# Layer 1's preparation in a four-layer graph network: fillings for TensorE, and the order of DVE's and GpSimd's first work

## The chip, the cores and the metric

One core of a Trainium2 chip runs the whole program in one launch. The time is device microseconds (us) of that core; a smaller number is better. Engines are called PE or TensorE (matrix products), DVE or VectorE, ACT or ScalarE, POOL or GpSimd, and SP, which issues most DMAs.

## The reference, cut to what matters

x has 3327 nodes of 64 values, adj is 3327 x 3327. Four layers follow one another, each ending in a layer norm of x plus the layer's result. Layer 1, where the change lies:

```python
x = _layernorm(x + _L0_gnn_ref(L0_gnn_t, x, adj))           # layer 0: leaves a centred, scaled x
# layer 1
x_tan = _logmap0(x, C)
left  = x_tan @ att_W[:D] + att_b
right = x_tan @ att_W[D:]
adj_att = sigmoid(left + right.T) * adj                      # N x N
x_local = _logmap(x[:, None, :], x[None, :, :], C)           # N x N x 64, never formed by the kernel
support_t = einsum('ij,ijd->id', adj_att, x_local)
x = _layernorm(x + _proj(_expmap(x, support_t, C), C))
# layer 2: two rounds of tanh([adj @ x, x] @ W); layer 3: a ranked, decayed neighbour sum
```

For an x whose rows all have enough variance, layer 0's result lies at one distance from the origin. The kernel then takes the logarithm as a cubic in one product of rows, so that layer 1 is, for every pair of a block of neighbours j and a chunk of nodes i: a product of rows (pq), a sigmoid times adj, the cubic, and a second product that sums over j.

## The kernel before, in words

The nodes are padded to 26 blocks of 128 and paired into 13 "slots by two": block b lies in slot 2b for b below 13, and block b + 13 in slot 2b + 1. A tile [128, 26, 64] holds one row of 64 per node and slot.

**Preparation, first part** (lines 918 to 1008, in an order written out by hand for all engines). DVE sums and centres x (xc). TensorE turns x to columns (pt_x) and multiplies each pair of blocks by the centred attention weights, so pr holds each node's left and right term; the 13 products lie in four groups of 4, 4, 4 and 1 (`turned`). Between them stand products whose result nobody reads, the fillings (`idle`, an identity times a matrix of 128x512 or 128x256). n_low counts rows with a low variance. DVE copies it to `flag`; every engine loads the flag and branches on it (lines 1819 and 1820) before layer 1's main part. DVE also forms lf (left), rb (right plus bias), s, ga, gas and others, each [128, 26]. GpSimd has put x minus its last column into lj.

**Preparation, second part** (`near_sphere`, from line 1244, again in a written order). DVE multiplies rows of lj by s (`scaled`, which takes b and n and does slots 2b to 2(b + n)), and makes the rows ri (`rows_of_i`). TensorE turns lf, lj and ri into columns, in tiles of PSUM, and ScalarE or DVE copies them out: `left` gives lb, a row of lf on all partitions; `right` gives ljT[0]; `wrong` gives the other half order ljT[1]; `turn` gives riT. `bank` and `alone` issue TensorE's instructions at once and return the function that copies. The tile `after` is a copy of one column that GpSimd makes so as to wait for DVE.

**Main loop.** 52 pairs of a j block and a half of the columns, each in two steps, 104 steps in all. `attention` makes a sigmoid on ScalarE (L1076) and its product with adj on GpSimd (L1088); the very first pair is done in two halves, and `next(start)` issues the first. `products` makes pq (L1103) three steps ahead; `linear` makes a on DVE (L1115) and a square on ScalarE (L1116); `gather` makes v on DVE (L1124) and sums on TensorE (L1133). One step thus needs two DVE instructions, one square, half a sigmoid, half a GpSimd product and eight TensorE records.

The blocks of adj come by DMA on SP's queue: four of them are kept in SBUF from the start, the others pass through a ring of four.

In the first part the lines that the change touches are 977 to 1008, in the second 1262 to 1275:

Of the kernel before, what the change touches and what calls it, by code (L numbers as in the profile page):

```python
# [10 lines left out]
F32 = mybir.dt.float32  # L11
# [4 lines left out]
ALU = mybir.AluOpType  # L16
# [3 lines left out]
P = 128  # L20
N = 3327
NB = 26
NP = NB * P
D = 64
# [34 lines left out]
LOG_NORM = float(np.arctanh(np.float64(ATANH_MAX)))  # L59
# [17 lines left out]
def kernel(  # L77
# [11 lines left out]
    nc = tc.nc  # L89
# [14 lines left out]
    ident = const.tile([P, P], F32, name="ident")  # L104
    make_identity(nc, ident)
    lj = const.tile([P, NB, D], F32, name="lj")
# [9 lines left out]
    ones = const.tile([P, 1], F32, name="ones")  # L116
# [4 lines left out]
    attb_sb = const.tile([P, 1], F32, name="attb_sb")  # L121
# [69 lines left out]
    center_4 = center.unsqueeze(1).to_broadcast([P, 4, P])  # L191
# [705 lines left out]
    with tc.tile_pool(name="l1", bufs=1) as l1:  # L897

        def l1_stat(name):
# [6 lines left out]
        s, inv_s, gas, dl, al, xf, lf, rb = (  # L906
            l1_stat(name) for name in ("s", "inv_s", "gas", "dl", "al", "xf", "lf", "rb")
        )
# [4 lines left out]
        r2 = l1.tile([P, 2, NB], F32, name="r2")  # L913
        flag = l1.tile([1, 1], I32, name="flag")
        xc = xpool.tile([P, NB, D], F32, tag="x", name="xc")
        vec, sca = nc.vector.tensor_tensor, nc.vector.tensor_scalar
        stt = nc.vector.scalar_tensor_tensor
        with tc.tile_pool(name="l1a", bufs=1) as l1a, tc.tile_pool(
            name="l1ap", bufs=1, space=PSUM
        ) as l1ap:  # L920
            v = l1a.tile([P, NB], F32, name="v")
            sums = l1a.tile([P, NB], F32, name="sums")
            sq = l1a.tile([P, NB, D], F32, name="sq_c")
            xT = l1a.tile([P, HALF], F32, name="xT_0")

            idle = l1ap.tile([P, 4 * P], F32, name="idle")
            for _ in range(3):
                nc.tensor.matmul(idle, ident, center_4, start=True, stop=True)  # L928

            pw = l1ap.tile([P, 4], F32, name="pw")  # L930
            attw_c = l1a.tile([P, 4], F32, name="attw_c")
            halves = (slice(0, None, 2), slice(1, None, 2))
            for h in halves:
                nc.vector.tensor_reduce(sums[:, h], x0[:, h, :], axis=AX.X, op=ALU.add)
            for h in halves:
                stt(
                    xc[:, h, :], sums[:, h].unsqueeze(2).to_broadcast([P, NBH, D]), -1.0 / D,
                    x0[:, h, :], op0=ALU.mult, op1=ALU.add,
                )
            for h, c in zip(halves, (x0, xc)):  # L940

                nc.gpsimd.tensor_tensor(
                    lj[:, h, : D - 1], c[:, h, : D - 1],
                    c[:, h, D - 1 : D].to_broadcast([P, NBH, D - 1]), ALU.subtract,
                )

            pr = l1ap.tile([P, NBH, 2, 2], F32, name="pr")
            turned = []
            for i, g in enumerate(range(0, NBH, 4)):
                n = min(4, NBH - g)  # L950
                pt = l1ap.tile([P, 4 * P], F32, tag="pt", bufs=4, name=f"pt_x_{g}")
                for k in range(n):
                    nc.tensor.transpose(
                        pt[:, k * P : (k + 1) * P],
                        by_half(x0)[:, g + k].rearrange("p h d -> p (h d)"), ident,
                    )
                if i == 1:
                    nc.tensor.matmul(pw, center, attw_dg, start=True, stop=True)
                    nc.scalar.copy(attw_c, pw)
                    for h in halves:  # L960
                        nc.scalar.activation(sq[:, h, :], xc[:, h, :], AF.Square)
                nc.scalar.copy(xT[:, g * P : (g + n) * P], pt[:, : n * P])
                turned.append((g, n))
            for h in halves:
                nc.vector.tensor_reduce(v[:, h], sq[:, h, :], axis=AX.X, op=ALU.add)
            sca(vq[:, 1], v, 0.81 / D, LN_EPS, ALU.mult, ALU.add)
            sca(vq[:, 0], v, MIN_VAR, None, ALU.max)
            sca(vq[:, 2], v, 0.81 / D - 0.81, LN_EPS, ALU.mult, ALU.add)

            low = stat("low")  # L970
            stt(low, v, NEAR_VAR, real, op0=ALU.is_lt, op1=ALU.mult)
            lows = small.tile([P, 1], F32, tag="lows", name="lows")
            nc.vector.tensor_reduce(lows, low, axis=AX.X, op=ALU.add)
            root = l1a.tile([P, 2, NB], F32, name="root")
            n_low = l1ap.tile([1, 1], F32, name="n_low")
            for i, (g, n) in enumerate(turned):
                if i == 3:
                    nc.tensor.matmul(n_low, lows, ones, start=True, stop=True)
                for k in range(g, g + n):
                    nc.tensor.matmul(  # L980
                        pr[:, k].rearrange("p h t -> p (h t)"), xT[:, k * P : (k + 1) * P],
                        attw_c, start=True, stop=True,
                    )
                if i in (0, 3):
                    w = 2 if i else 4
                    nc.tensor.matmul(
                        idle[:, : w * P], ident, center_4[:, :w], start=True, stop=True
                    )
            nc.scalar.activation(root, vq[:, :2], AF.Sqrt)
            nc.scalar.activation(warm, ones, AF.Sigmoid)  # L990
            nc.vector.reciprocal(root, root)
            t = l1a.tile([P, 2, NB], F32, name="t")
            vec(t, vq[:, :2], root, ALU.mult)
            nc.vector.tensor_copy(flag, n_low)
            vec(t, t, root, ALU.mult)
            stt(r2, t, -3.0, root, op0=ALU.add, op1=ALU.mult)
            prs = pr.rearrange("p n h t -> p (n h) t")
            stt(lf, prs[:, :, 0], -0.5 * LOG_NORM, r2[:, 0], op0=ALU.mult, op1=ALU.mult)
            stt(rb, prs[:, :, 1], -0.5 * LOG_NORM, r2[:, 0], op0=ALU.mult, op1=ALU.mult)

            nc.vector.reciprocal(rq, vq[:, 1:])
            sca(rb, rb, attb_sb, None, ALU.add)
            sca(s, r2[:, 1], -0.45, None, ALU.mult)
            vec(g1, vq[:, 2], rq[:, 0], ALU.mult)
            vec(ga, vq[:, 1], rq[:, 1], ALU.mult)
            sca(aa, g1, -1.0, 1.0, ALU.mult, ALU.add)
            vec(gas, ga, s, ALU.mult)
            sca(lj[:, :, D - 1], aa, 1.0, None, ALU.add)
        in_order.close()

        def near_sphere(mT, ljT_0, xm, sq_e, t_e, rows_63):
# [3 lines left out]
            with tc.tile_pool(name="n1", bufs=1, reuse_waits="tile") as n1, tc.tile_pool(  # L1015
                name="n1w", bufs=2, reuse_waits="tile"
            ) as n1w, tc.tile_pool(
                name="n1c", bufs=1, space=PSUM, reuse_waits="tile"
            ) as n1c, ExitStack() as pairs:
                first_ps = ExitStack()  # L1020
                n1p = first_ps.enter_context(
                    tc.tile_pool(name="n1p", bufs=1, space=PSUM, reuse_waits="tile")
                )
# [4 lines left out]
                ri = mT.rearrange("p (n d) -> p n d", d=D)  # L1028
# [171 lines left out]
                def made(pt, make, b, n, at_once=True):  # L1200
                    dst, src = make(pt, b, n)

                    def copy(to=nc.scalar.copy):
                        to(dst, src)
                        if make is right and b < 9:
                            if at_once:
                                change_over(b, n)
                            else:
                                changes.append((b, n))

                    return copy
# [20 lines left out]
                def alone(make, b, n):  # L1232

                    pt = n1p.tile([P, 4 * P], F32, name=f"first_{make.__name__}_{b}")
                    return made(pt, make, b, n)

                with tc.manual_schedule(
# [7 lines left out]
                    def scaled(b, n):  # L1245

                        sl = slice(2 * b, 2 * (b + n))
                        vec(
                            lj[:, sl, : D - 1], lj[:, sl, : D - 1],
                            s[:, sl].unsqueeze(2).to_broadcast([P, 2 * n, D - 1]), ALU.mult,  # L1250
                        )
# [7 lines left out]
                    rows_of_i(4, 8)  # L1259
                    scaled(5, 4)  # L1260
                    rows_of_i(8, NBH)
                    scaled(0, 5)

                    nc.gpsimd.tensor_scalar(
                        al, ga, CUBIC_PLUS, CUBIC_SHIFT - CUBIC_ROOT, ALU.mult, ALU.add
                    )

                    after = n1.tile([P, 1], F32, name="after")
                    nc.gpsimd.tensor_copy(after, lj[:, 0, :1])
                    spread_a, spread_b = bank(0, left, 0, 4), bank(1, left, 13, 4)  # L1270
                    spread_a()
                    spread_b()
                    start = attention(0)
                    next(start)
                    rows_j = alone(right, 9, 4)
                    spread_c = alone(left, 4, 3)
                    spread_d = alone(left, 17, 3)
                    spread_c()
# [36 lines left out]
                    for t in range(len(tiles)):  # L1315
# [24 lines left out]
                        if t == len(tiles) - 3:  # L1340
                            pq = n1q.tile([P, 2, 512], F32, tag="pq", name="pq_early")
                            pm = pq[:, :, : 3 * (P + 2)].rearrange("p a (k w) -> p a k w", k=3)
                            for b in range(6):
                                nc.tensor.matmul(
                                    pm[:, b // 3, b % 3], mT[:, b * P : (b + 1) * P], all_m,
                                    start=True, stop=True,
# [530 lines left out]
```

## Time and profile before

| | us |
|---|---|
| median of 3 runs | 555.25 (553.59 to 555.3) |
| profiled execution | 554.5 |
| its span, first to last instruction | 552.8 |
| TensorE busy | 524.6 (95%) |
| DVE busy | 373.2 (68%) |
| ScalarE busy | 275.2 (50%) |
| GpSimd busy | 207.6 (38%) |

One profiled execution was recorded instruction by instruction. A row of the timeline gives the start and length of an instruction or of a run of equal ones, its engine, line, operation, what it writes and reads, and the shape; a bracket holds the idle time of its engine before it and the work whose end is taken to have ended it. An fp32 product shows as two records on TensorE. PEclk is the share of its full clock that TensorE was granted. The mean over the span is 0.983. Layer 1's preparation fills the first 23 us, its loop the time to about 224 us.

### The profile page before, as it was taken

To read this page: it belongs to the slowest core of one execution; us is meant where nothing else is said; L and a number is where in the kernel's file an instruction comes from. 1 tells how busy PE (TensorE), PEld (TensorE's weight loads), DVE (VectorE), ACT (ScalarE), POOL (GpSimd) and SP (SyncE) were. 2 spreads that over 40 slices of the span, in tenths; PEclk is the share of its full clock that TensorE was granted. 3 is DMA by queue.
4 is the path that set the end of the run, shared out by engine and by line. 5 is a ranking of instruction groups with operands and counts; after the bars stand their busy time and mean duration, and the time that the engine had idled before them with its cause. 6 is when DMAs were issued, how large, how long until landed. Compare 5 with 4: busy or idle time off the path is not lost.

```text
span 552.8 us, 7387 instructions
## 1 busy us (share of the span) xinstructions
PE 524.6 (95%) x2841; PEld 228.6 (41%) x2841; DVE 373.2 (68%) x553; ACT 275.2 (50%) x321; POOL 207.6 (38%) x85
## 2 busy tenths in 40 slices
PE   8879999999999999999999999999999999989991
PEld 5622222222222222854444444444455555645551
DVE  6789999999999999899000011200679769697733
ACT  4699999999999997620000100000365333433321
POOL 3599999999999999000000000000001000000000
PEclk9799999999999999899999999999999999999996
DMA  8979667666777626699999049999019994799601
GB/s 288 341 225 301 219 224 234 212 233 208 232 240 225 209 95 277 247 427 427 421 430 395 3 167 422 429 420 383 32 53 362 323 375 140 238 295 354 244 1 37
DMA packets 33892, 143.56 MB, mean 260 GB/s; under 512 B 10269, under 2 KB 11959, under 8 KB 28855
## 3 DMA queue, kind: packets, MB, share of 16 engines
q1 hardware_dynamic: 31511, 142.40, 69.9%
q10 hardware_dynamic: 2336, 0.59, 0.5%
q8 instruction: 24, 0.39, 0.3%
q14 instruction: 21, 0.17, 0.1%
HBM read 141.53 MB, written 0.87 MB: 258 GB/s over the span
## 4 chain that ended last, share of the span: by engine, by line
PE 66%; DVE 16%; ACT 11%; issue 5%; DVEq 0%; POOL 0%; ACTq 0%; POOLq 0%
PE cnt L421 26%; PE cnt L526 11%; DVE v L1124 8%; PE pq L1103 7%; PE acc L722 6%; ACT pq L1116 5%; ACT sg L1076 5%; PE acc L1133 4%; PE acc L737 3%; DVE a L1115 2%; DVE w L539 1%; DVE mask L341 1%; PE cnt L412 1%; PE idle L928 1%; PE pm L1416 1%
## 5 line engine op out<-in xcount | busy, mean ns | idle before, releaser
L1088 POOL TENSOR_TENSOR sg<-sg,at 128x1664 f32<-128x1664 f32 x44 | 163.9, 3751 | 2.0 <-ACT sg L1076 1.9
L1103 PE MATMUL pq<-riT,ljT 64*128 64x416 f32 x416 | 100.8, 561 | 10.3 <-DVE v L1124 6.2
L1116 ACT ACTIVATE pq<-pq,al,ga 128x832 f32<-128x832 f32 x104 | 104.7, 1011 | 11.0 <-DVE a L1115 11.0
L1124 DVE SCALAR_TENSOR_TENSOR v<-pq,a 128x832 f32<-128x832 f32 x104 | 105.4, 1014 | 3.6 <-ACT pq L1116 2.5
L1115 DVE SCALAR_TENSOR_TENSOR a<-pq,sg 128x832 f32<-128x832 f32 x104 | 105.2, 1012 | 0.5 <-PE prep_fours L1194 0.5
L1133 PE MATMUL acc<-v,xv 128*64 128x416 f32 x416 | 95.3, 537 | 0.0
L1076 ACT ACTIVATE sg<-lb,rb 128x1664 f32<-128x1664 f32 (+1 forms) x53 | 87.2, 1647 | 0.0
L541 ACT ACTIVATE w<-cnt 128x832 int16<-128x832 f32 x55 | 47.2, 862 | 71.2 <-PE cnt L526 71.1
L421 PE MATMUL cnt<-at_l,lj 128*64 128x416 f32 x448 | 80.3, 513 | 0.0
L653 POOL TENSOR_TENSOR s<-sq,s 128x384 bf16<-128x384 f32 (+1 forms) x4 | 4.1, 1024 | 197.9 <-ACT s L652 197.9
L506 ACT ACTIVATE x<-cnt 128x416 f32<-128x416 f32 x8 | 4.1, 517 | 130.6 <-PE cnt L421 130.6
L1103 PEld LDWEIGHTS pq<-riT,ljT 64*128 64x128 f32 x416 | 31.3, 184 | 83.7 <-DVE v L1124 82.8
L539 DVE TENSOR_SCALAR w<-cnt 128x832 int16<-128x832 f32 x49 | 50.1, 1022 | 21.2 <-PE cnt L526 20.8
L526 PE MATMUL cnt<-mask,rest 128*128 128x416 bf16 x200 | 51.5, 339 | 2.4 <-ACT w L541 1.4
L526 PE MATMUL cnt<-mask,tri 128*128 128x416 bf16 x208 | 53.5, 339 | 0.1
L722 PE MATMUL acc<-w,s 128*128 128x416 bf16 x208 | 52.5, 339 | 0.5 <-DVE hid L794 0.5
L421 PEld LDWEIGHTS cnt<-at_l,lj 128*64 128x64 f32 x448 | 31.9, 137 | 46.1 <-issue 45.2
L1133 PEld LDWEIGHTS acc<-v,xv 128*64 128x64 f32 x416 | 20.6, 134 | 61.7 <-issue 58.0
L341 DVE TENSOR_SCALAR mask<-ah 128x1664 bf16<-128x1664 f32 x42 | 43.5, 1035 | 1.0 <-DMA ah<-in_adjT 1.0
L409 DVE COPY lj<-pn_l 128x512 f32<-128x512 f32 (+1 forms) x4 | 2.4, 592 | 60.8 <-PE pn_l L373 60.8
L421 PE MATMUL cnt<-kept,lj 128*64 128x416 f32 x224 | 41.2, 513 | 0.0
L1088 POOL TENSOR_TENSOR sg<-sg,kept 128x1664 f32<-128x1664 f32 (+1 forms) x10 | 30.0, 3026 | 0.8 <-ACT sg L1076 0.8
(291 smaller groups left out, 413.8 us busy)
## 6 DMA issues: line engine op xcount, KB each, us to landing
at_l<-in_adjT SPq DMA_DIRECT2D x24, 1664.0 KB, 12.2
at<-in_adjT SPq DMA_DIRECT2D x44, 832.0 KB, 5.0
ah<-in_adjT SPq DMA_DIRECT2D x42, 832.0 KB, 6.5
bt_l<-in_adjT SPq DMA_DIRECT2D x8, 1664.0 KB, 16.7
kept<-in_adjT SPq DMA_DIRECT2D x7, 1664.0 KB, 9.2
lb<-lf_rows SPq DMA_DIRECT2D x2, 384.0 KB, 6.3
ljT<-ljT SPq DMA_DIRECT2D x4, 128.0 KB, 2.3
x<-in_x ACTq DMA_DIRECT2D x1, 416.0 KB, 5.4
```

Source lines behind the costliest of these rows:

```text
L341: nc.vector.tensor_scalar(mask[q], at, 0.0, None, ALU.not_equal)
L421: nc.tensor.matmul(acc[c][h * D : (h + 1) * D, :], hw[:, slot(jb), :], blocks[jb][:, o : o + CW], start=c not in begun, stop=last, skip_gr ...
L526: nc.tensor.matmul(cnt[c][:, e, :], mat, mask[q][:, of], start=start, stop=(mat is tri), skip_group_check=True,)
L539: nc.vector.tensor_scalar(w.bitcast(I16), cnt[c], 0.0, None, ALU.max)
L722: nc.tensor.matmul(acc[h, c][:, e, :], s12[:, slot(jb)].rearrange("p t d -> p (t d)"), ws[q, c][:, e, :], start=first, stop=last,)
L1076: nc.scalar.activation(sg[:, :, of], lbs[:, :, of], AF.Sigmoid, bias=rb[:, sl : sl + 1])
L1088: nc.gpsimd.tensor_tensor(sg[:, :, of], sg[:, :, of], at[:, :, of], ALU.mult)
L1103: nc.tensor.matmul(pq[:, h, :], ljT[h != jb // NBH][rows, of], riT[rows, ch * CW : (ch + 1) * CW], start=True, stop=True,)
L1115: stt(a_s[t], pqs[t], CUBIC_PLUS, us.pop(t), op0=ALU.add, op1=ALU.mult)
L1116: nc.scalar.activation(pqs[t], pqs[t], AF.Square, bias=al[:, one], scale=ga[:, one])
L1124: stt(w, pqs.pop(t), CUBIC_REST, a_s.pop(t), op0=ALU.add, op1=ALU.mult)
L1133: nc.tensor.matmul(accs[cp, ci][h * D : (h + 1) * D, :], xv[:, slot(jb), :], w[:, h, :], start=(jb == orders[cp][0]), stop=(jb == orders[c ...
```

## The change

In the first part, n_low is multiplied after the second group and no longer ahead of the fourth; a filling of 128x512 follows the first, second and fourth group (before: 128x512 after the first, 128x256 after the fourth); and DVE forms lf, rb and rb plus bias after the other small tiles and no longer ahead of them. In the second part, the last rows of lj (slots 0 to 9) are multiplied by s in ten instructions of one slot each, with s as a scalar for each partition, and no longer in one instruction with s as a spread tensor; GpSimd's copy `after` reads the last rows of ri and no longer lj; and a filling of 128x512 goes into the tile of the first `right` ahead of it, which its turnings then overwrite.

```diff
             for i, (g, n) in enumerate(turned):
-                if i == 3:
-                    nc.tensor.matmul(n_low, lows, ones, start=True, stop=True)
                 for k in range(g, g + n):
...
-                if i in (0, 3):
-                    w = 2 if i else 4
-                    nc.tensor.matmul(
-                        idle[:, : w * P], ident, center_4[:, :w], start=True, stop=True
-                    )
+                if i == 1:
+                    nc.tensor.matmul(n_low, lows, ones, start=True, stop=True)
+
+                if i != 2:
+                    nc.tensor.matmul(idle, ident, center_4, start=True, stop=True)
...
-            prs = pr.rearrange("p n h t -> p (n h) t")
-            stt(lf, prs[:, :, 0], -0.5 * LOG_NORM, r2[:, 0], op0=ALU.mult, op1=ALU.mult)
-            stt(rb, prs[:, :, 1], -0.5 * LOG_NORM, r2[:, 0], op0=ALU.mult, op1=ALU.mult)
 
             nc.vector.reciprocal(rq, vq[:, 1:])
-            sca(rb, rb, attb_sb, None, ALU.add)
...
             sca(lj[:, :, D - 1], aa, 1.0, None, ALU.add)
+            prs = pr.rearrange("p n h t -> p (n h) t")
+            stt(lf, prs[:, :, 0], -0.5 * LOG_NORM, r2[:, 0], op0=ALU.mult, op1=ALU.mult)
+            stt(rb, prs[:, :, 1], -0.5 * LOG_NORM, r2[:, 0], op0=ALU.mult, op1=ALU.mult)
+            sca(rb, rb, attb_sb, None, ALU.add)
...
                     rows_of_i(8, NBH)
-                    scaled(0, 5)
+                    for k in range(10):
+                        one = slice(k, k + 1)
+                        sca(lj[:, k, : D - 1], lj[:, k, : D - 1], s[:, one], None, ALU.mult)
...
-                    nc.gpsimd.tensor_copy(after, lj[:, 0, :1])
+                    nc.gpsimd.tensor_copy(after, ri[:, NB - 1, :1])
...
-                    rows_j = alone(right, 9, 4)
+                    pt = n1p.tile([P, 4 * P], F32, name="first_right_9")
+                    nc.tensor.matmul(pt, ident, center_4, start=True, stop=True)
+                    rows_j = made(pt, right, 9, 4)
```

## The prediction

> **What bounds the kernel now.** I read the busy table and the slices first: TensorE is busy 95% of the 552.8 us span, so what delays its first product of layer 1's main loop delays the end. Then the waits and the timeline of layer 1's preparation, 7 to 28 us. From 34 us on the loop runs DVE at one instruction per 0.93 us with hardly a gap, TensorE at 0.97 + 0.92 us per step and GpSimd at 3.75 us per two steps: three engines tied. No later part has room for a late or early start, so I count a shift of the loop's start one for one at the end.
>
> The TensorE timeline (start, length, what; a bracket holds the idle time before and who ended it):
> ```profile
> 10.16 1.10 PE L986 MATMUL idle<-both_m,ident 128*128 128x512 f32 x2
> 13.10 0.19 PE L978 MATMUL n_low<-ones,lows 128*1 128x1 f32 x2
> 13.46 0.68 PE L986 MATMUL idle<-both_m,ident 128*128 128x256 f32 x2
> 14.36 1.43 PE L1148 MATMUL prep_left<-ident,lf 128*128 128x128 f32 x8 [0.22 <-DVE rb L999]
> 16.62 1.11 PE L1170 MATMUL first_right<-ident,lj 128*128 128x128 f32 x4 [0.83 <-DVE lj L1248]
> 17.52 1.49 PE L1148 MATMUL first_left<-ident,lf 128*128 128x128 f32 x6
> 19.80 1.98 PE L1180 MATMUL first_wrong<-ident,lj 128*64 128x128 f32 x16
> 23.23 0.97 PE L1103 MATMUL pq<-riT,ljT 64*128 64x416 f32 x4
> ```
> After 14.36 TensorE waits once, 0.83 us for DVE's first product with s; the rest is work in order. The loop starts at 23.23. The clock shows why that work is slow (stretch, length, TensorE busy, PEclk, DMA share, GB/s):
> ```profile
> 8.06:11.47 3.41, 3.41 (x27) 1.00 1.00 422
> 11.47:14.88 3.41, 3.19 (x27) 1.00 0.95 379
> 14.88:18.29 3.41, 2.58 (x13) 0.50 1.04 325
> 18.29:21.71 3.42, 3.42 (x25) 0.50 0.99 397
> 21.71:25.12 3.41, 3.30 (x23) 1.00 0.97 387
> ```
> From 14.88 to 21.71 the clock is half: a 128x128 turning product takes 0.21 us (first_left, six starts in 1.28) against 0.11 later (prep_fours, x4 in 0.60 with its tail). DVE and GpSimd run beside it:
> ```profile
> 15.88 0.68 DVE L1248 TENSOR_TENSOR lj<-lj,s 128x504 f32<-128x504 f32 x1 [0.60 <-POOL tri L1608]
> 19.49 0.81 DVE L1248 TENSOR_TENSOR lj<-lj,s 128x630 f32<-128x630 f32 x1
> 20.44 0.19 POOL L1269 COPY after<-lj 128x1 f32<-128x1 f32 x1 [4.48 <-DVE lj L1248]
> 20.58 1.94 POOL L1088 TENSOR_TENSOR sg<-sg,kept 128x832 f32<-128x832 f32 x1
> 23.37 13.16 POOL L1088 TENSOR_TENSOR sg<-sg,kept 128x832 f32<-128x832 f32 x5 [0.85 <-ACT sg L1076]
> ```
> GpSimd's first product ends at 22.52; its second waits 0.85 us for ScalarE's second sigmoid, which stands behind first_wrong's copy. So first_wrong, not the first product, sets GpSimd.
>
> **What the Trainium skill says.** "TensorE: Matmul & The Clock Gate", Part 1: the clock is half by default, a free-running window of about 3.4 us decides, busy gives full clock, idle takes it. The trace agrees: half clock from 14.88 to 21.71, twice 3.41; and the idle products before 8 us take 0.91 a record (5.49 for six) against 0.55 later, though the view has no record of the clock there and shows 1.00. The stretch that lost the clock was 3.19 us busy by the table, but with products of 4 columns; wide ones and turnings fill about 1.0 us of it (0.43 idle, 0.5 prep_left). So narrow products hardly count. Stretch 14.88 to 18.29, 2.58 busy, did not win it back; 18.29 to 21.71, full, did. "SBUF — State Buffer", Who interferes with whom: DVE in a two-port mode, or with two SBUF inputs, and a reading GpSimd instruction exclude each other, the second waits for all of the first. The trace shows it in layer 3: GpSimd's L653 at 409.31 for 0.91, and
> ```profile
> 409.40 1.70 DVE L341 TENSOR_SCALAR mask<-ah 128x1664 bf16<-128x1664 f32 x1
> 411.96 1.01 DVE L341 TENSOR_SCALAR mask<-ah 128x1664 bf16<-128x1664 f32 x1
> ```
> 0.69 longer. "VectorE: DVE Perf Modes", What auto-detection actually checks: one source and the destination in SBUF, outermost counts even or equal, give the two-port mode. The ten new instructions (63 to 63, fp32) fit that; no trace here shows one of 63.
>
> **The change, part by part.**
> (1) n_low after group 1. It needs lows, which DVE ends at 12.57; TensorE is through group 1 at 12.13 and stands 0.5 us. n_low at 12.63 instead of 13.10, so flag at about 13.10 instead of 13.32. SP's two kept loads go out some 0.2 earlier, into a DMA already at 0.95 to 1.0: nothing.
> (2) Fillings. Before 512 + 256 wide (1.10 + 0.68); after three of 512. Second idle 12.74 to 13.80, groups 2 and 3 (ten records of 0.11) to 14.93, last pr finished at 15.07 against 13.60. Third idle from 14.93.
> (3) lf, rb, rb + b behind the rest. DVE's r ends at 13.66, rq to lj[63] fill 13.55 to 14.66, then lf waits for pr: 15.10, rb 15.20, rb + b 15.42 (0.1 an instruction, 0.2 where one needs the last). The branch follows as now (scaled(9,4) 0.80 after the last start): 16.22 instead of 15.88, **+0.34 for all of DVE's stream**.
> (4) A 512 filling ahead of first_right: 1.06 at full clock, 1.83 at half (six records in 5.49 before 8 us).
> (5) scaled(0,5), 0.81 us, becomes ten instructions. Nearest row: 128x26 by scalar, 0.08 to 0.1 apart. Ten: 1.0, from 19.83 to about 20.9 if nothing blocks.
> (6) GpSimd waits for rows_of_i(8,13) (end 19.91) and no longer for scaled(0,5). Its product could start at 20.2; the sigmoid ahead of it decides (below). DVE and GpSimd now overlap: some five of the ten are done by then, the others wait for its end at 22.2 and end at 22.75. Bounds: 20.9 and 22.75. I take the late one, by row 409.40. Behind them on DVE stands the copy of first_turn, for which pq waits (rows: copy 22.39 to 23.08, pq 23.23).
>
> **Does the clock hold?** In stretch 11.47 to 14.88 there is then 0.85 us of wide product (the second idle's columns; the third starts at 14.93) and no turning: no more than the 1.0 that lost it. I expect half clock from 14.88 again. But from 14.93 TensorE is full without the 0.83 us hole, so the clock returns at 18.29, not 21.71. The chain:
> - third idle 14.93 + 1.83 = 16.76; prep_left 8 x 0.21 to 18.4 (before 15.6 + tail);
> - full clock: filling 1.0 to 19.4; first_right 0.45 to 19.85; first_left 0.66 to 20.5; first_turn 0.45 to 20.95; first_wrong 1.0 (half of 1.98) to 21.95; second turn 0.45 to 22.4; few 0.33, fours 0.45 to 23.2; pq at **23.3**, or **23.55** with the blocked DVE (copy 22.75 to 23.45).
> ScalarE: second lb copy ends 19.2 (now 16.4), first sigmoid 19.25 to 20.25, so GpSimd's product at 20.3, 0.3 earlier than now; copies to 22.4; first_wrong's to 22.95; second sigmoid to 23.85, 0.5 later than now. GpSimd's second product moves with it; its pair for step 4 ends at 32.8 while DVE takes it at 33.97, so 1.2 us of slack covers that.
> Against 23.23: +0.1 to +0.35. **Sum: the fillings cost 2.5 us of TensorE work at the clock it meets, the earlier full clock gives nearly the same back.** I take +0.3.
>
> The profiled execution took 554.5 us: 552.8 of span and 1.7 around it; so 554.8 after. The median shown is 0.75 above that, so I forecast **555.5**.
>
> **Rivals.**
> - **Clock kept.** The window is free-running; if its edge falls so that two fillings lie in one, or the limit is lower than I read, TensorE stays at full clock: third idle to 15.99, left 16.9, filling 17.95, right, left, turn, wrong, turn to 20.95, few and fours 21.75, pq at 21.9: 1.3 us sooner, 554.2 on the median's scale, if DVE is not blocked; blocked, pq at 23.5. For it: 8.06 to 11.47 kept the clock with one 512 idle and turnings. Against: the same stretch as before holds no more. 0.22.
> - **Half clock throughout (slower).** The clock comes back at 21.71 as before, or later, since a window that begins before 14.93 is not full: then filling 18.5 to 20.3, right to 21.15, left 22.05, turn, wrong, turn 23.95, few and fours 24.75, pq at 24.9: +1.7, **557.0**; if half clock reaches the first pq (0.97 each becomes 1.9), +3, 558.3. It decides when the return is later than about 21.5. For it: 2.58 of 3.41 busy was not enough before. Against: TensorE has no wait from 14.93. 0.22.
> - **The single slots do not get beside GpSimd.** Either they wait (in my sum), or GpSimd waits until 20.9, which the second sigmoid hides. The part brings nothing: 555.2 to 555.6. 0.12.
> - My own case: 0.44.
>
> **How the numbers follow.** 0.3% is 1.7 us, about what a measurement of this kernel can tell from no change. Own case and blocked slots lie within it. "Clock kept" ends mostly within it and passes it only where the runs' own spread (553.59 to 555.3) helps: 0.1 faster. Half clock is mostly beyond: 0.22 slower, with the tail of the own case. Same 0.68. Range 553.7 to 557.4: it takes in the kept clock and the half clock at 557.0, and leaves out the longer half clock.
>
> **What would show it.** Right: n_low near 12.6, lf near 15.1, scaled(9,4) near 16.2, prep_left near 16.8 and slow, PEclk 0.50 for one window of 3.4 us instead of two, first_right near 19.4, pq at 23.2 to 23.6; some of the ten slots long or late while L1088's first product runs. Wrong: PEclk at 1.00 from 14 to 22 with pq near 21.9, or 0.50 beyond 21; ten slots done by 21; a loop whose end does not move with its start.

## The result, and the profile after

| | before | after |
|---|---|---|
| median of 19 runs each | 554.66 (552.37 to 556.61) | 556.2 (555.2 to 562.74) |
| ratio to before, 95% interval | | 1.0064 (1.0043 to 1.0085) |
| profiled execution | 554.5 | 562.31 |
| its span | 552.8 | 560.1 |

The change made the kernel **slower**, by 0.64%. A ratio lies near the quotient of the means (here 557.85 and 554.46) and not of the medians, and it leaves out runs over 1.5% above the fastest of their kernel, of which only e3 below has any (4 of 20).

The runs of the changed kernel lie in groups: 12 of 19 at 555.2 to 556.3, two at 558.15 and 558.49, five at 562.15 to 562.74. These five carry about half of the 3.4 us between the means; the other 14 lie 1.8 us above before. The one execution that was profiled belongs to the last group. The profile below therefore shows a loss of 7.8 us, not the 1.5 of the median.

TensorE's timeline of the changed kernel, the rows that answer to those of before:
```profile
9.43 1.10 PE L986 MATMUL idle<-both_m,ident 128*128 128x512 f32 x2
12.17 0.19 PE L983 MATMUL n_low<-ones,lows 128*1 128x1 f32 x2 [0.21 <-DVE lows L973]
14.28 1.10 PE L986 MATMUL idle<-both_m,ident 128*128 128x512 f32 x2
15.49 1.06 PE L1146 MATMUL prep_left<-ident,lf 128*128 128x128 f32 x8
17.25 0.60 PE L1168 MATMUL first_right<-ident,lj 128*128 128x128 f32 x4
18.87 1.09 PE L1178 MATMUL first_wrong<-ident,lj 128*64 128x128 f32 x16
21.77 0.30 PE L1168 MATMUL prep_fours<-ident,lj 128*128 128x128 f32 x1 [0.89 <-DVE lj L1262]
25.51 0.47 PE L1168 MATMUL prep_fours<-ident,lj 128*128 128x128 f32 x1 [3.44 <-DVE lj L1262]
27.56 0.80 PE L1168 MATMUL prep_fours<-ident,lj 128*128 128x128 f32 x2 [1.58 <-DVE lj L1262]
28.57 1.76 PE L1101 MATMUL pq<-riT,ljT 64*128 64x416 f32 x4 [0.21 <-DVE riT L1202]
```
All of this trace stands some 0.4 us earlier than before's (lows ended at 12.57 there; here n_low, which waits for lows, starts at 12.17). Up to first_wrong TensorE is ahead by over half a microsecond and at full speed. Then it waits three times, 5.9 us in all, for single slots of lj, and pq comes at 28.57 where it stood at 23.23.

The cause stands in the timelines of DVE and GpSimd, in the same stretch:
```profile
19.19 8.64 DVE L1262 TENSOR_SCALAR lj<-lj,s 128x63 f32<-128x63 f32 x10
27.75 0.68 DVE L1202 COPY riT<-first_turn 128x512 f32<-128x512 f32 x1
19.61 7.69 POOL L1086 TENSOR_TENSOR sg<-sg,kept 128x832 f32<-128x832 f32 x4
36.34 7.41 POOL L1086 TENSOR_TENSOR sg<-sg,kept 128x1664 f32<-128x1664 f32 x2 [9.05 <-ACT sg L1074]
```
Ten instructions take 8.64 us. For the tile lj alone between 19.66 and 27.2, and for sg between 19.4 and 27.5, the trace gives (x count: shortest, median, longest in ns; first and last start):
```profile
L1262 DVE TENSOR_SCALAR lj<-lj,s x5: 246/1971/2018, 19.5 to 25.4; 128x63 f32<-128x63 f32 x5
L1086 POOL TENSOR_TENSOR sg<-sg,kept x4: 1938/1944/1959, 19.6 to 25.4; 128x832 f32<-128x832 f32 x4
```
Four slots last about 1.97 us each, as long as a GpSimd product; each begins within 0.1 us of one product's start and ends within 0.1 us after its end. A free slot takes 0.25. So DVE and GpSimd take turns: a slot waits for all of a running product, is let in, and the next product begins at the same time and holds up the next slot. Below, what the two engines exclude each other from is called the port, and this row of waits the jam.

The jam ends only when GpSimd has no sigmoid left. ScalarE's timeline says why it has no more:
```profile
20.50 2.56 ACT L1074 ACTIVATE sg<-lb,rb 128x832 f32<-128x832 f32 x2
31.57 1.02 ACT L1114 ACTIVATE pq<-pq,al,ga 128x832 f32<-128x832 f32 x1 [8.27 <-DVE a L1113]
```
The third pair's sigmoid stands behind the square, the square waits for DVE's a, and a stands behind the ten slots. GpSimd, which took the port, is starved by it in the end: 9.05 us idle before 36.34.

The clock (stretch, length, TensorE busy, PEclk, DMA share, GB/s):
```profile
13.39:16.80 3.41, 3.31 (x22) 1.00 1.03 322
16.80:20.22 3.42, 3.42 (x35) 1.00 1.00 420
20.22:23.64 3.42, 0.96 (x8) 1.00 0.97 402
23.64:27.05 3.41, 0.47 (x1) 0.50 0.58 235
27.05:30.46 3.41, 2.69 (x7) 0.50 0.01 5
30.46:33.88 3.42, 3.42 (x12) 0.50 0.00 0
```
It was kept through the preparation, and lost by the jam itself: after a stretch with 0.96 of 3.42 busy it is half from 23.64 to 33.88, so the first pq takes 1.76 instead of 0.97. The bill of this execution: pq comes 5.34 later; two pq at half clock add 2 x 0.79, and the first v of the loop starts at 34.15 against 27.22, 6.93 later; the second v, for which the square on ScalarE is late, at 37.21 against 29.92, 7.29 later. The last v of the layer starts at 230.39 against 223.04, 7.35 later, and the span is 7.3 longer. Nothing of it is given back in the loop.

### The profile page after: what moved, and what is told of

It is laid out like the page before. It is cut to its first block, busy times and chain, and to the rows that moved or that the text cites. A ratio compares the mean times of both kernels' runs of the same rounds, so it can differ in the third digit from the quotient of the medians.

```text
span 560.1 us, 7403 instructions
## 1 busy us (share of the span) xinstructions
PE 525.0 (94%) x2845; PEld 226.4 (40%) x2845; DVE 381.5 (68%) x562; ACT 275.4 (49%) x321; POOL 207.6 (37%) x85
## 4 chain that ended last, share of the span: by engine, by line
PE 60%; DVE 20%; ACT 11%; issue 6%; DMA 1%; DVEq 0%
PE cnt L421 25%; PE cnt L526 11%; DVE v L1122 9%; PE pq L1101 7%; PE acc L722 6%; ACT pq L1114 5%; ACT sg L1074 5%; PE acc L737 3%; PE acc L1131 2%; DVE a L1113 2%; DVE lj L1262 2%; DVE w L539 1%; DVE mask L341 1%; PE cnt L412 1%; DMA x<-in_x 1%
## 5 line engine op out<-in xcount | busy, mean ns | idle before, releaser
L1101 PE MATMUL pq<-riT,ljT 64*128 64x416 f32 x416 | 102.4, 569 | 10.0 <-DVE v L1122 6.0
L539 DVE TENSOR_SCALAR w<-cnt 128x832 int16<-128x832 f32 x49 | 50.1, 1023 | 21.9 <-PE cnt L526 21.7
```

The source lines that it names most:

```text
L539: nc.vector.tensor_scalar(w.bitcast(I16), cnt[c], 0.0, None, ALU.max)
L1101: nc.tensor.matmul(pq[:, h, :], ljT[h != jb // NBH][rows, of], riT[rows, ch * CW : (ch + 1) * CW], start=True, stop=True,)
```

## The experiments

Three questions: what costs the 7 us (A), what decides whether an execution pays it (B), and what is left to gain (C). They were timed in four sets, each beside before, whose median in them was 554.71 (e1 to e4), 553.94 (e5, e6, a_again), 554.09 (e7 to e9) and 554.81 (e10, e11).

### A. What the ten slots wait for

**e3_slots_only**: before, with the slots and GpSimd's order alone; no fillings, nothing moved in the first part.
```diff
-                    scaled(0, 5)
+                    for k in range(10):
+                        one = slice(k, k + 1)
+                        sca(lj[:, k, : D - 1], lj[:, k, : D - 1], s[:, one], None, ALU.mult)
-                    nc.gpsimd.tensor_copy(after, lj[:, 0, :1])
+                    nc.gpsimd.tensor_copy(after, ri[:, NB - 1, :1])
```


> The kernel before with two edits alone: the ten slots, and GpSimd's copy reading ri. Fillings, n_low and lf as before. Lock theory with the clock as the switch: in executions at half clock the second sigmoid comes late (about 22), so that only the first product is in the way and a few slots go between the first and second; the ten end near 22 to 24, 0 to 1.5 us slower than before. In executions at full clock several products stand ready and it is 4 to 7 us slower. Clock theory: no slower than before.

Measured: 561.71 (554.54 to 563.97), ratio 1.008 (1.0052 to 1.0109): 8 of 20 runs at 554.5 to 557.3, 12 at 560.9 to 564. This part alone makes a loss and groups of times. Its profile is of the low group (557.27), with the clock half from 12.78 to 19.60:
```profile
19.02 5.13 DVE L1264 TENSOR_SCALAR lj<-lj,s 128x63 f32<-128x63 f32 x10
19.43 1.97 POOL L1088 TENSOR_TENSOR sg<-sg,kept 128x832 f32<-128x832 f32 x1
22.15 5.75 POOL L1088 TENSOR_TENSOR sg<-sg,kept 128x832 f32<-128x832 f32 x3 [0.75 <-ACT sg L1076]
```
Here GpSimd stood 0.75 us without a sigmoid after its first product. In that gap DVE did slots at 0.16 us each, and two of the ten waited, not four. No execution of its upper group was profiled.

**e1_behind**: the changed kernel, with the tile `after` read from lj[:, 9, :1], so that GpSimd starts behind all ten slots.

> The changed kernel with one edit: the copy that holds GpSimd reads slot 9 of lj, so its first product starts behind all ten slots and nothing of the ten overlaps it. Lock theory (each GpSimd product lets one of the ten through): the ten end within 1.8 us of their start, pq starts at 21.0 to 21.8 us, the time is 1.5 to 2.5 us below the kernel before (ratio 0.995 to 0.998). Clock theory (the fillings and the later lf cost the time): still slower than before by 1 us or more. Small-instruction theory (ten instructions cost more than one by themselves): as the clock theory, with the ten taking 5 us or more though nothing else runs.

Measured: 556.1 (553.3 to 558.55), 1.0028 (1.0015 to 1.0042). No slot waits any more, and no run lies above 558.6:
```profile
20.33 1.70 DVE L1262 TENSOR_SCALAR lj<-lj,s 128x63 f32<-128x63 f32 x10
22.32 7.86 POOL L1086 TENSOR_TENSOR sg<-sg,kept 128x832 f32<-128x832 f32 x4
24.25 0.97 PE L1101 MATMUL pq<-riT,ljT 64*128 64x416 f32 x4
```
That it would beat before was wrong, it is slower: in its profile the clock is half from 12.25 to 19.08, and pq comes at 24.25. The jam is one loss, the clock another.

**e2_one**: after, with `scaled(0, 5)` in the place of the ten; GpSimd still ahead.

> The changed kernel with the ten slots put back into one instruction of 630 elements with two SBUF inputs, GpSimd's first product still ahead in the written order. Lock theory: the one instruction is issued right behind the rows of ri, some 0.3 us before the product, so it takes the lock first and the product waits; at worst it waits for one product, 1.95 us. The time lies 0.5 to 2.5 us below the kernel before. Clock theory: slower than before by 1 us or more. If overlap as such costs (whatever the count of instructions), it is as slow as the changed kernel.

Measured: 555.17 (552.31 to 557.33), 1.0017 (1.0 to 1.0033). The gain of 0.5 to 2.5 us that was expected is not there. Its profile is of its fastest execution, at full clock: DVE's one instruction starts at 19.08, GpSimd's product at 19.90 behind it, pq at 21.33. One instruction can be in time, or wait once; ten offer nine more places to wait.

**e6_second_behind**: after, with a copy of lj[:, 9] on GpSimd ahead of its second product only.

> The changed kernel with one more copy on GpSimd, ahead of its second product, that reads slot 9 of lj: the first product still overlaps the ten, the second waits for them. Lock theory: one slot waits for one product, so the ten end near 22.1 and pq starts near 22.8, in every execution: 5 us below the slow executions of the changed kernel, 0 to 1 us below the kernel before, with a spread of 2 us and not of 7. Clock theory: no gain over the changed kernel.

Measured: 556.42 (555.52 to 557.48, 9 runs), 1.0047 (1.0028 to 1.0066). One slot waits (20.14 to 22.15), the ten are done at 22.96; the upper groups are gone, the spread is 2 us. But it is slower than before, where 0 to 1 us less was expected, and its mean lies 1.2 us above that of e5 below, in which no slot waits.

**a_again**: after once more, for the profile of another execution.

> The changed kernel once more, for a second profile. Its times stood in groups: 555.2 to 556.3, 558.2 to 558.5 and 562.2 to 562.7. Lock theory: in an execution of the low group one product alone stands in the way, because the clock went to half near 14 to 15 us and the second sigmoid came late; the ten then end 2 to 4 us after their start instead of 8.6. If this execution is of the high group, it looks like the first profile.

Measured: 557.76, between the groups. Its clock is half from 12.18 to 22.42:
```profile
19.93 1.92 PE L1276 MATMUL first_right<-both_m,ident 128*128 128x512 f32 x2
20.93 3.44 DVE L1262 TENSOR_SCALAR lj<-lj,s 128x63 f32<-128x63 f32 x10
21.86 1.97 POOL L1086 TENSOR_TENSOR sg<-sg,kept 128x832 f32<-128x832 f32 x1 [0.48 <-ACT sg L1074]
26.20 0.97 PE L1101 MATMUL pq<-riT,ljT 64*128 64x416 f32 x4
```
The same program, with a slow TensorE: the second sigmoid is late, only one product is ready, one slot waits. That wait costs nothing here: the ten end at 24.37, and the copy of riT behind them waits for TensorE until 25.36. Over these profiles one slot waits in a_again and e6, two in e3 and four in after: about 2 us for each product that stands ready while slots are left.

**e5_psum**: after, with one instruction in place of the ten that reads s from PSUM, so that it has one input in SBUF.
```diff
-                    for k in range(10): ...
+                    few = n1c.tile([P, 4 * P], F32, tag="acc1", name="prep_few")
+                    s_few = few[:, 3 * P : 3 * P + 10]
+                    sca(s_few, s[:, :10], 1.0, None, ALU.mult)
+                    vec(
+                        lj[:, :10, : D - 1], lj[:, :10, : D - 1],
+                        s_few.unsqueeze(2).to_broadcast([P, 10, D - 1]), ALU.mult,
+                    )
```


> The changed kernel with the ten slots made by one instruction whose s comes from PSUM (a copy of s for slots 0 to 9 lies in an unused quarter of a PSUM tile), so that it has one SBUF input and no two-port mode; GpSimd's first product runs beside it. Lock theory: the instruction takes 0.8 us though the product is running, pq starts near 21.3, 1.5 to 2.5 us below the kernel before. If any DVE instruction on SBUF waits for GpSimd, it takes 2 us or more.

Measured: 556.17 (552.67 to 557.46), 1.0019 (1.0002 to 1.0036). The instruction took 0.81 us (19.70 to 20.51) beside a product that began at 20.15: no wait. "The Trainium skill", "SBUF — State Buffer", Who interferes with whom, says that a DVE instruction with at most one input in SBUF, outside the two-port modes, does not contend; here it did not. The gain of 1.5 to 2.5 us stayed away all the same: the clock was half from 14.59 to 18.00, and pq came at 23.30. That leaves the fillings and the clock.

### B. The clock

**e4_fill_only**: before, with all of the change but the slots and GpSimd's order.

> The kernel before with the first part's edits (fillings, n_low, lf and rb later) and the filling ahead of the first right, and with the one instruction and GpSimd behind it as before. Lock theory: 1 to 2.5 us below the kernel before, since the clock is kept in most executions and nothing blocks; as fast as the run with the ten slots behind which GpSimd waits, within 0.5 us. Clock theory: slower than before by 1 us or more.

Measured: 555.62 (552.33 to 558.44), 1.0011 (0.9998 to 1.0023): not to be told from before, where 1 to 2.5 us less was expected. Its profile (554.64):
```profile
14.59 2.06 PE L986 MATMUL idle<-both_m,ident 128*128 128x512 f32 x2
16.75 1.67 PE L1146 MATMUL prep_left<-ident,lf 128*128 128x128 f32 x8
18.25 1.02 PE L1274 MATMUL first_right<-both_m,ident 128*128 128x512 f32 x2
23.29 0.97 PE L1101 MATMUL pq<-riT,ljT 64*128 64x416 f32 x4
```
This is the chain of the prediction: half clock for one window (14.59 to 18.00), prep_left at 16.75 (forecast 16.76), pq at 23.29 (23.3). The fillings do not hold the clock safely, and what they cost is too small to tell here.

**e7_wide_before** and **e8_wide_after**: to set the clock by other means, the attention weights are padded from 4 to 96 columns with zeros. Each product of pr then streams 96 columns; the next overwrites all but 4 of them. The same edit in before and in after:
```diff
-            attw_c = l1a.tile([P, 4], F32, name="attw_c")
+            attw_c = l1a.tile([P, 96], F32, name="attw_c")
+            nc.gpsimd.memset(attw_c, 0.0)
-            pr = l1ap.tile([P, NBH, 2, 2], F32, name="pr")
+            pr_w = l1ap.tile([P, 4 * NBH + 92], F32, name="pr")
+            pr = pr_w[:, : 4 * NBH].rearrange("p (n h t) -> p n h t", h=2, t=2)
...
-                    nc.scalar.copy(attw_c, pw)
+                    nc.scalar.copy(attw_c[:, :4], pw)
...
-                        pr[:, k].rearrange("p h t -> p (h t)"), xT[:, k * P : (k + 1) * P],
+                        pr_w[:, 4 * k : 4 * k + 96], xT[:, k * P : (k + 1) * P],
```


> The kernel before, with the attention weights padded from 4 to 96 columns by zeros: each of the 13 products pr now writes 96 columns, of which the next overwrites all but its first 4. A record of pr costs 0.11 us for its weights whatever its width up to there, so TensorE's time stays and the columns that it streams rise from 4 to 96 a record. Clock theory in its new form (columns streamed in a window of 3.4 us keep the clock, narrow products do not): the clock stays at 1.00 from about 8 us to the end of the preparation in all or nearly all executions, pq starts near 21.2, and the median falls by 1.5 to 2.5 us. If instructions count and not columns, or if the extra columns cost time, no gain.

Measured: 552.88 (552.41 to 554.44), 0.9982 (0.9968 to 0.9996), faster than before, by less than the 1.5 to 2.5 us expected. The clock is 1.00 all through the preparation:
```profile
10.68 2.02 PE L982 MATMUL pr<-attw_c,xT 128*128 128x96 f32 x16 [0.36 <-ACT xT L964]
20.70 0.97 PE L1105 MATMUL pq<-riT,ljT 64*128 64x416 f32 x4
```
In before, sixteen records of these products with 4 columns took 1.95 us and did not hold the clock; with 96 they take 2.02 and do. All five profiles with the padding keep the clock until the preparation ends (e7 to e11), two of the nine without it do (after, e2). The closest pair: e3's window from 9.36 to 12.78, without the padding, is 2.88 us busy and loses the clock; e7's from 9.58 to 13.00 is 3.06 us busy and keeps it. And e7's next window keeps it with only 1.99 of 3.41 us busy, where before lost it with 3.19. "The Trainium skill", "TensorE: Matmul & The Clock Gate", Part 1, says that the chip watches how busy TensorE is and counts no instructions; the trace agrees, and adds that the time which the profile shows as busy does not decide by itself: products that stream few columns need not count.

> The changed kernel with the same padding of the attention weights. Lock theory with the clock as its switch: with the clock kept in all or nearly all executions the high group becomes the rule, four slots wait for four products, and the median goes UP to 561.5 to 563 although TensorE works faster. If the three groups of times had another cause, the groups stay as they were or the median falls.

Measured: 563.19 (562.76 to 564.01, 5 runs), 1.0178 (1.0156 to 1.0199). Every run is now in the upper group:
```profile
19.55 8.60 DVE L1264 TENSOR_SCALAR lj<-lj,s 128x63 f32<-128x63 f32 x10
19.97 7.65 POOL L1088 TENSOR_TENSOR sg<-sg,kept 128x832 f32<-128x832 f32 x4
28.90 1.76 PE L1103 MATMUL pq<-riT,ljT 64*128 64x416 f32 x4 [0.22 <-DVE riT L1204]
```
**A kept clock is enough for the jam in after.** The edit that makes before faster makes after slower: with the clock kept (in this profile from 7.60 to 24.67), the left rows are turned early, the first sigmoids come early, and GpSimd's four products follow one another while the slots wait. Whether it is needed is not shown. In e3 12 of 20 runs lie in the upper group, while of before's 65 runs in the same set only 13 have a mean clock of 0.988 or more (e2's profile, with the clock kept, has 0.989). Some executions of e3 probably jam with the clock lost for part of the preparation.

**e9_ten_psum**: e8 with ten instructions, still one for each slot, but with s read from PSUM as in e5.

> The changed kernel with the padding, and with each of the ten slots multiplied by an s that lies in PSUM, so one SBUF input and no two-port mode; count, size and place as in the change. Lock theory: none of the ten waits, they stand 0.16 to 0.2 us apart beside GpSimd's running product, the high group is gone, the median is 7 to 10 us below that of the changed kernel with the padding and at or below the kernel before. If it is the count of small instructions beside GpSimd, it stays at 558 or more.

Measured: 553.65 (552.49 to 555.82), 0.9994 (0.9981 to 1.0006), 9.5 us below e8:
```profile
19.32 1.38 DVE L1278 TENSOR_TENSOR lj<-lj,prep_few 128x63 f32<-128x63 f32 x10
19.52 15.09 POOL L1088 TENSOR_TENSOR sg<-sg,kept 128x832 f32<-128x832 f32 x6
```
Ten instructions in 1.38 us beside six products without a pause. So it is not the number of instructions, but what their form shares with GpSimd.

### C. What is left

**e10_wide_psum**: before, with the padding, s from PSUM in one instruction, and GpSimd's `after` reading ri; no new fillings, nothing moved in the first part. **e11_wide_fill**: e4 with the padding.

> A version that may beat both: the kernel before with the padded attention weights, the last rows times s in one instruction with s from PSUM, and GpSimd's first product ahead of it; none of the new fillings. Lock theory: nothing waits; GpSimd's first product starts near 19.3 instead of 20.1, the wait of 0.18 us for it at the second a goes, and the median is 0 to 0.6 us below that of the kernel before with the padding (552.9): 552.3 to 552.9.

Measured: 552.53 (552.33 to 552.99, 7 runs), 0.9953 (0.9937 to 0.9969): faster than before, 2.3 us below its median in the same set, with a spread of 0.7 us.
```profile
19.30 0.81 DVE L1279 TENSOR_TENSOR lj<-lj,prep_few 128x630 f32<-128x630 f32 x1
19.50 15.05 POOL L1090 TENSOR_TENSOR sg<-sg,kept 128x832 f32<-128x832 f32 x6
21.11 0.97 PE L1105 MATMUL pq<-riT,ljT 64*128 64x416 f32 x4
```
GpSimd's first six products run without a gap, and DVE's instruction beside the first of them takes its usual 0.81 us.

> The kernel before with the padding and with the change's fillings and order in the first part, the one instruction and GpSimd behind it as before. It prices the fillings where the clock is kept in any case: pq starts near 21.3 instead of 20.7, so the median is 0.5 to 0.9 us above that of the kernel before with the padding: 553.4 to 553.8. If the fillings still served the clock, it would be as fast or faster.

Measured: 552.89 (552.25 to 553.94, 12 runs), 0.9965 (0.9951 to 0.9978), with pq at 21.67. Against e7 (pq at 20.70) the expected 0.5 to 0.9 us is not there. The two were timed on different chips, and their intervals overlap, so the times can't settle it. The traces tell more: e7's pq comes 0.97 earlier, but its second a then waits 0.18 for GpSimd, and the first v starts at 24.98 against 25.45 in e11, the last v of the layer at 220.70 against 221.13. Some 0.4 us are left, and behind the layer these two executions differ by 0.8 the other way. In the same way e10's pq is 0.41 later than e7's, for TensorE waits 0.66 for DVE's instruction, but GpSimd is ready: the first v starts at 24.70, the last at 220.58. In the traces e10 is thus 0.1 to 0.3 us ahead of e7. The times of the two (0.9953 and 0.9982), again from different chips, do not separate how much of e10's gain is the port and how much the padding.

## Why the prediction failed

The forecast was 555.5, no change that can be measured. The median came out 0.7 above that and inside the range, but the kernel is measurably slower, and a quarter of its runs lie far beyond 557.4.

**The step that failed is (6), in its upper bound and in its own words** "some five of the ten are done by then, the others wait for its end at 22.2 and end at 22.75". It took the lock as one wait, after which DVE has the port to itself for the rest. The row it rested on (mask at 409.40, 0.69 longer) has one DVE instruction beside one GpSimd instruction and can't show what follows when both have more. The runs show the port changing hands slot by slot: the term is not one product's end but 2 us for each product ready, up to four, and the last slot ends at 27.83 instead of 22.75. That the second comer waits for the whole of the first, as the prediction says, held. What was missing was to count the instructions on both sides. This step explains the upper group and the loss in e3; it is not shown to be the whole of what the other 14 runs lose.

The other points:
- **(1) to (3), right or nearly.** On before's scale (0.4 added) n_low stands at 12.57 (forecast 12.63), lf at 14.86 (15.10), scaled(9,4) at 15.98 (16.22). The delay of DVE's stream is then about 0.1, not 0.34: the second filling and the ten records after it took 1.99 us at full clock (12.29 to 14.28), where the sum has 2.19.
- **(4), right.** A filling took 1.02 to 1.13 at full clock against 1.06, and 1.92 to 2.08 at half against 1.83. The closing sum "cost 2.5 us of TensorE work" does not follow from the terms above it (1.06, 1.83 and 1.0 more, 0.68 less: 3.2); the 23.3 comes from the chain and does not rest on it.
- **(5), 0.7 short where nothing waits.** Free slots start 0.16 us apart, so ten span 1.7 (e1) and not 1.0; this is small beside the waits.
- **The clock, right in kind.** e4 and e5 lose it for exactly one window and bring pq to 23.29 and 23.30. But the window's edge falls elsewhere from execution to execution: after's profile and e2's keep the clock through the preparation, e1 loses it for two windows and a_again for three. Two of the seven profiles with the fillings and no padding keep it, so 0.22 for this case was not far off; what was wrong is its price.
- **The rival "clock kept"** was right by itself: pq at 21.9 forecast, 21.33 in e2, whose trace runs 0.5 ahead of before's. (Its 554.2 takes the 1.3 us off the forecast of 555.5; off before's 555.25 it is 553.9.) Its blocked form was priced at 23.5 and came at 28.57, by the same step (6). The prediction treated an early TensorE as a gain only; it did not ask what GpSimd does with sigmoids that come earlier. It had seen that the second sigmoid "stands behind first_wrong's copy" and left this out of the kept-clock case.
- **The slower rival, half clock throughout,** was the right sign for another reason. Its mechanism occurs (a_again: half to 22.42, pq at 26.20, forecast 24.9), but the 562 us that were profiled come from the opposite, the clock kept.
- **"The single slots do not get beside GpSimd"** named the mechanism with 0.12 and held that the part "brings nothing". It brings a loss: e3, with this part alone, is at 1.008.

**What is not settled:** the lower group of after, 12 runs around 556, was never profiled itself. That its 1.5 us above before are a blocked slot and the fillings together is argued from e6 (one slot waits, 556.42) and e4 (1.0011), not shown. e1, in which no slot waits, is slower than before too (1.0028), with a profile that loses the clock for two windows; how many executions of after do so is not on record.

## What to carry to other kernels

When an instruction is split so that DVE and GpSimd may run side by side, ask first whether its form and GpSimd's exclude each other; if they do, price the split as the smaller of the two counts of ready instructions times GpSimd's instruction, not as one wait. Reading one operand from PSUM took the waits away for 0.16 us of copying. And price every edit twice, with an upstream engine early and late: here the same ten instructions took 3.4 us in an execution with TensorE's clock at half and 8.6 in one with it full.

## What the runs showed of the hardware that was not expected

- While both had instructions ready, DVE and GpSimd took turns instruction by instruction, and DVE alone paid: in after and e8 four slots of 0.25 us each waited out a product of 1.9 us, while four products took 7.69 and 7.65 us, and 7.86 in e1, where no slot stands between them.
- The fp32 form of 63 to 63 elements with a scalar for each partition is one that waits: the slots issued beside a running product lasted 1.94 to 2.02 us (after, a_again, e3, e6, e8). "The Trainium skill", "VectorE: DVE Perf Modes", What auto-detection actually checks, lets an outermost count that is equal on both sides pass for the two-port mode, so this is the likely reason; no run here separates it from s being read from SBUF as well.
- Zero columns served for the clock: 24 times the columns in each product of pr cost 0.07 us per sixteen records (2.02 against 1.95), and the clock stayed full through the preparation in the profiles of e7 to e11.
